# A decoder layer on one core: attention's logits in single PSUM banks, separate rings for weights and maxima, half products, and mask with maximum in one VectorE instruction

## Chip, cores and metric

One core of a Trainium2 chip runs the whole layer in one launch. The metric is device time in microseconds (us), the median of the runs shown; before the change it is 2776.85 us (three runs, 2776.67 to 2789.18). The profile is one further execution of the same kernel, with its own time.

## What is computed

The input x has 4 sequences of 1024 tokens with 256 features, and there is a context of 4 times 154 tokens. Three blocks follow each other, each with a residual:

```
x = x + liquid_scan_block(layernorm(x))
x = x + cross_attention(layernorm(x), ctx, ctx)          # 16 heads of 16, 154 keys
x = x + transformer_block(layernorm(x))                  # causal, 16 heads of 16, 1024 keys; then a mixture of experts

scores = q @ k.T / sqrt(16);  scores = where(causal, scores, -inf)   # the mask only in the transformer block
attn = softmax(scores);  o = attn @ v
w = softmax over the 2 best of 8 router logits
moe = sum_e w[e] * (gelu(h2 @ w1[e] + b1[e]) @ w2[e] + b2[e])
```

The large products are fp32. The kernel takes the softmax with the true row maximum subtracted.

## The kernel before

**Stages.** The scan block comes first (lines 166 to 574), then both attentions in one program whose TensorE order is written out by a planner (lines 600 to 1214), then the experts (lines 1230 to 1342), where the tokens, sorted by expert in DRAM, are taken in 39 blocks of 256.

**One unit of attention** is one sequence, one half of it (512 queries, called a block), and one group c of four heads out of sixteen. Heads lie 32 rows apart, so the four heads of a group are the four 32-row strips of TensorE, and two heads make a pair (strips 0 and 1, or 2 and 3). There are 32 units of cross-attention with 4 weight steps each, and 32 of self-attention, 16 with 8 steps (first half of a sequence) and 16 with 16 steps (second half). A unit has two lists of steps:

- *Maximum steps*, `few` (line 728, cross-attention) and `many` (line 744, self-attention). The logits of one pair are computed with queries on the partitions into a tile `ps_max` of two PSUM banks, one bank per head (lines 735 and 750). `many` adds the causal mask to the last 128 columns of both heads (line 755). Then VectorE reduces both heads in one instruction to the negated maximum (lines 739 and 757). `put` (line 759) transposes the four maxima of a unit and adds them to the queries as a seventeenth feature (line 766, tile `qs`), so that the second product yields logits less their maximum.
- *Weight steps*, `logits` (line 805). For a block kt of 128 keys (77 in cross-attention) and one pair, the logits are computed with keys on the partitions into a tile `ps_exp`, again two banks (line 814). ScalarE takes the exponential of both banks in one instruction into `pt` (line 816), and on the diagonal GpSimd zeroes what lies above it (line 820).
- *Products*, `weigh` (line 781): once both pairs of a key block have been issued, four matmuls, one per head, multiply `pt` with the values into the bank `ps_o` (line 788).

**PSUM.** `ps_max` and `ps_exp` share one tag, `sc`, with three tiles of two banks (line 603): six banks. `ps_o` has one bank, and one bank `mm` (line 609) serves every other matmul of attention: projections, transposes, output products, the router.

**The planner** (lines 1127 to 1214). It walks the weight steps; k counts them within a unit, so an even k is the first pair of a key block and an odd k the second. After each weight step it emits maximum steps of the next unit (`find`), kept LEAD = 3 steps ahead, so that a weight step is followed by a maximum step of the other pair. Then `fill` may emit filler: jobs of the queues `ahead` (what the next group of units needs: norms, projections) and `behind` (what follows a finished unit: `back`, output products, router), each with a lag in steps, and at most one job with matmuls per call. If `find` has just emitted a `put`, that `fill` is skipped. After an odd step it also calls `weigh` and then `fill` once more:

```
some = find(near - (near - far) * (k + 1) // n + LEAD)
left = n - k + sum(len(units[x][1]) for x in range(u + 1, limit)) - LEAD
if not some:
    fill(left)
if k % 2 and len(waiting) > 1:
    weigh()
    fill(left)
```

TensorE runs in exactly this order; ScalarE, VectorE and GpSimd are ordered by the framework's scheduler. When a group's first maxima come up, `all_ahead` emits at once what is left of `ahead`.

**Router and experts.** `route` (line 956) computes the router's logits, the gates and each token's place, and scatters the rows to DRAM. Its last four jobs per block add the experts' second bias: `turned` (line 1002) transposes the gates, `biases` (line 1008) multiplies them with the 8x256 table `eb2`, and VectorE adds the result to the residual (line 1015). In the expert loop SyncE issues for each block xr, w1, w2 and bias (lines 1312 to 1318); `results` (line 1290) computes the second product of the block before, copies it to `y` (line 1295) and scatters it.

## Time and profile before

| | us |
|---|---|
| median of three runs (2776.67 to 2789.18) | 2776.85 |
| the profiled execution | 2801.33 |
| its span, first to last instruction | 2799.6 |

| stage, from the start of the span | from | to |
|---|---|---|
| scan | 0 | 720 |
| cross-attention | 720 | 1075 |
| self-attention | 1075 | 2085 |
| last block's router, then experts | 2085 | 2800 |

| engine | busy us | share of the span | instructions |
|---|---|---|---|
| PE (matmul) | 2482.2 | 89% | 13678 |
| DVE (VectorE) | 1427.0 | 51% | 2902 |
| ACT (ScalarE) | 934.6 | 33% | 1410 |
| POOL (GpSimd) | 396.4 | 14% | 560 |

A group line of the profile reads: source line, engine, operation, tile written<-tiles read, shapes, count | busy us, mean ns of one | idle us of the engine just before them, and what ended it. A timeline line reads: start, length, engine, line, operation, tiles, shapes, count merged. An fp32 matmul of the program shows as two MATMUL records, so the two heads of a pair are four. Matmul ends are modelled, so a busy PE is not PE at its peak.

### The profile page before, as it was taken

How to read it: one execution, taken by the hardware profiler on the slowest of the kernel's cores; microseconds unless marked ns; L12 is line 12 of the kernel's file. 1: busy time of each engine (PE TensorE's matmuls, PEld its weight loads, DVE VectorE, ACT ScalarE, POOL GpSimd, SP SyncE). 2: the span in 40 equal slices, each digit the busy share in tenths (PEclk: the TensorE clock that was granted, in tenths of full speed). 3: DMA queues.
4: the chain of work that ended last, by engine and by line, in shares of the span. 5: the costliest groups of instructions: out<-in, count | busy, mean ns of one | idle time of the engine just before them, and what ended most of it. 6: DMA issues, size and time to landing. Idle time of an engine off the chain costs nothing. (4 is left out here: it accounts for less than half of the span.)

```text
span 2799.6 us, 36302 instructions
## 1 busy us (share of the span) xinstructions
PE 2482.2 (89%) x13678; PEld 1446.6 (52%) x13678; DVE 1427.0 (51%) x2902; ACT 934.6 (33%) x1410; POOL 396.4 (14%) x560
## 2 busy tenths in 40 slices
PE   5999999995898998989999999999886999999990
PEld 2666666554444554433433344333334888888880
DVE  4667766657556555575757576567733111111113
ACT  2444333432454543333423423352341222222220
POOL 1110000001101000122213131213212111111110
PEclk9999999997899999997979879897897999999995
DMA  4595000001000010100011001100003454554435
GB/s 100 112 240 138 0 1 1 0 1 26 22 19 16 22 27 16 32 11 16 8 30 40 1 10 29 39 1 24 24 1 135 166 183 167 174 187 157 172 128 181
DMA packets 138001, 186.01 MB, mean 66 GB/s; under 512 B 33513, under 2 KB 108636, under 8 KB 137820
## 3 DMA queue, kind: packets, MB, share of 16 engines
q1 hardware_dynamic: 116028, 126.32, 14.5%
q0 software_dynamic: 15264, 51.00, 7.0%
q10 hardware_dynamic: 6528, 6.29, 0.7%
q8 instruction: 111, 1.82, 0.3%
q14 instruction: 70, 0.57, 0.1%
HBM read 110.93 MB, written 61.24 MB: 61 GB/s over the span
## 5 line engine op out<-in xcount | busy, mean ns | idle before, releaser
L816 ACT ACTIVATE pt<-ps_exp 128x1024 f32<-128x1024 f32 (+4 forms) x512 | 434.6, 862 | 642.1 <-PE ps_exp L814 492.8
L814 PE MATMUL ps_exp<-qs,kT 32*128 32x512 f32 (+4 forms) x2048 | 498.4, 596 | 33.9 <-DVE mpad L757 14.7
L750 PE MATMUL ps_max<-kT,qa 32*128 32x512 f32 (+3 forms) x1536 | 402.3, 620 | 22.8 <-ACT pt L816 16.2
L757 DVE TENSOR_REDUCE mpad<-ps_max 128x2 f32<-128x1024 f32 (+3 forms) x256 | 260.3, 1020 | 133.9 <-PE ps_max L750 130.9
L1222 PE MATMUL ps<-hT,w 128*128 128x256 f32 x1248 | 288.4, 385 | 23.3 <-ACT mid L1223 21.5
L814 PEld LDWEIGHTS ps_exp<-qs,kT 32*128 32x128 f32 (+1 forms) x2048 | 158.2, 190 | 269.9 <-issue 177.0
L1228 PE MATMUL ps<-w,mid 128*128 128x256 f32 x1248 | 287.7, 379 | 0.0
L1223 ACT ACTIVATE mid<-ps,bias 128x256 f32<-128x256 f32 x312 | 139.3, 472 | 435.2 <-DMA bias<-b1s 265.6
L1222 PEld LDWEIGHTS ps<-hT,w 128*128 128x128 f32 x1248 | 233.0, 191 | 71.9 <-ACT mid L1223 36.4
L788 PE MATMUL ps_o<-pt,vs 128*32 128x512 f32 (+4 forms) x2048 | 253.2, 567 | 0.3 <-ACT oT L796 0.3
L1228 PEld LDWEIGHTS ps<-w,mid 128*128 128x128 f32 x1248 | 234.4, 190 | 30.1
L820 POOL TENSOR_SCALAR_AFFINE_SELECT pt<-pt 128x256 f32<-128x256 f32 x256 | 103.4, 408 | 670.3 <-ACT pt L816 668.8
L1295 DVE COPY y<-ps 128x256 f32<-128x256 f32 x78 | 33.1, 425 | 309.0 <-PE ps L1228 309.0
L750 PEld LDWEIGHTS ps_max<-kT,qa 32*128 32x128 f32 x1536 | 133.7, 209 | 101.2 <-ACT pt L816 68.5
L755 DVE TENSOR_TENSOR ps_max<-ps_max,mask_qk 128x256 f32<-128x256 f32 x256 | 109.3, 429 | 123.9 <-PE ps_max L750 64.2
L739 DVE TENSOR_REDUCE mpad<-ps_max 128x4 f32<-128x616 f32 x128 | 101.8, 800 | 116.2 <-PE ps_exp L814 80.6
L1297 POOL DMA_INDIRECT parts<-y,to x78 | 75.8, 972 | 527.9 <-DVE y L1295 524.0
L308 PE MATMUL ps_xz<-xnT,w_in 128*128 128x512 f32 x256 | 125.2, 606 | 0.6 <-ACT xnT L300 0.6
L325 PE MATMUL ps_a<-w,w_a 128*128 128x512 f32 x256 | 123.7, 626 | 0.0
L1320 DVE CAST to<-xr 128x2 int32<-128x2 f32 x39 | 6.6, 169 | 206.7 <-DMA parts<-y,to 186.1
L788 PEld LDWEIGHTS ps_o<-pt,vs 128*32 128x32 f32 (+1 forms) x2048 | 42.2, 112 | 128.8 <-issue 98.3
L757 DVE TENSOR_REDUCE twice<-ps_max 128x2 f32<-128x1024 f32 (+3 forms) x128 | 105.0, 823 | 3.6
(263 smaller groups left out, 3190.7 us busy)
## 6 DMA issues: line engine op xcount, KB each, us to landing
w<-in_L_ffn_e_w_dram SPq DMA_DIRECT2D x78, 1024.0 KB, 5.9
routed<-zero POOLq DMA_DIRECT2D x16, 2080.0 KB, 64.3
xr<-routed SPq DMA_DIRECT2D x39, 260.0 KB
qa<-close SPq DMA_DIRECT2D x256, 32.0 KB, 2.0
xs<-in_x_dram SPq DMA_DIRECT2D x4, 1024.0 KB, 8.8
kT<-close SPq DMA_DIRECT2D x128, 32.0 KB, 2.0
plain<-row SPq DMA_DIRECT2D x8, 512.0 KB, 3.0
z<-parts SPq DMA_DIRECT2D x16, 256.0 KB, 3.5
```

The lines of the kernel that those rows point to most:

```text
L308: nc.tensor.matmul(ps, w_in[:, k, c * P : (c + 1) * P], xnT[:, k, :], start=k == 0, stop=k == 1)
L325: nc.tensor.matmul(ps, w_a[:, k, c * P : (c + 1) * P], w[:, k, :], start=k == 0, stop=k == 3)
L750: nc.tensor.matmul(ps[:, i, : s1 - s0], qT[r, j * P : (j + 1) * P], kT[r, c, s0:s1], start=True, stop=True)
L755: nc.vector.tensor_add(x, x, mask_qk.unsqueeze(1).to_broadcast([P, 2, P]))
L757: nc.vector.tensor_reduce(to, ps[:, :, : s1 - s0], AX.X, ALU.max, negate=True)
L788: nc.tensor.matmul(o[0][g * HP : (g + 1) * HP, off:], vs[:n, kt, (4 * c + g) * HV : (4 * c + g) * HV + HP], pts[g // 2][:n, g % 2, off:], ...
L814: nc.tensor.matmul(ps[:n, i, off:], kT[r, c, k0 : k0 + n], shifted[0][r, off:], start=True, stop=True)
L816: nc.scalar.activation(pt[:n, :, off:], ps[:n, :, off:], AF.Exp, scale=HD**-0.5)
L820: nc.gpsimd.affine_select(out=x, in_=x, compare_op=ALU.is_ge, fill=0.0, base=0, pattern=[[0, 2], [1, P]], channel_multiplier=-1,)
L1222: nc.tensor.matmul(ps, w1[:, k, f * P : (f + 1) * P], hT[:, k, :], start=k == 0, stop=k == 1)
L1223: nc.scalar.activation(mid[:, f, :], ps, AF.Gelu, bias=bias[:, f : f + 1])
L1228: nc.tensor.matmul(ps, mid[:, f, j * P : (j + 1) * P], w2[:, f, :], start=f == 0, stop=f == FF // P - 1)
```

## The change

- The tag `sc` becomes two tags, `max` and `exp`, with three tiles of one bank each. Every head has its own tile, so the exponential and the maximum are taken per head: two instructions of half the width in place of one.
- In `many`, the parts that end at the diagonal get mask and maximum in one VectorE instruction per head, over the part's whole width and with its result written back to PSUM; the mask is now 512 columns wide, zero but for the last 128. The maximum is no longer negated; the sign sits in `one16`, the constant row of the keys.
- `weigh` may do only the first 256 columns and leave the rest for its next call. That is allowed for key blocks between the first and the last of a unit that lie wholly below the diagonal, and is asked for when no filler is ready.
- The planner calls `weigh` after even steps, so a key block's product is issued one step sooner. After an even step `fill` is called only when work is crowded (always in cross-attention); after an odd step it is called once, and once more only behind a second half. `weigh` empties the jobs marked soon wherever they stand in `behind`.
- `turned`, `biases` and `eb2` go. In the expert loop each block loads its expert's second bias, spread over 128 partitions, as a fifth DMA on SyncE's queue, and the copy of line 1295 becomes an addition of it. (The other branch of the program, for ties in the router, gets the same bias; it isn't run here.)

```diff
-    mask_qk = const.tile([P, P], F32, name="mask_qk")
-    make_causal_mask(nc, mask_qk, mask_val=MASK)
+    mask_qk = const.tile([P, BLK], F32, name="mask_qk")
+    nc.gpsimd.memset(mask_qk[:, : BLK - P], 0.0)
+    make_causal_mask(nc, mask_qk[:, BLK - P :], mask_val=MASK)
...
-    nc.vector.tensor_reduce(one16, ident[:, HD::HP], AX.X, ALU.add)
+    nc.vector.tensor_reduce(one16, ident[:, HD::HP], AX.X, ALU.add, negate=True)
...
             def few(j0, pair):
-                ps = ps_s.tile([P, 2, BLK], F32, tag="sc", name="ps_max")
+                pss = [ps_s.tile([P, BLK], F32, tag="max", name="ps_max") for _ in range(2)]
...
-                nc.vector.tensor_reduce(
-                    m[:, j0 : j0 + 2, 2 * pair : 2 * pair + 2, HD].rearrange("p j i -> p i j"),
-                    ps[:, :, : 2 * n].rearrange("p i (j n) -> p i j n", n=n), AX.X, ALU.max, negate=True,
-                )
+                for i in range(2):
+                    nc.vector.tensor_reduce(
+                        m[:, j0 : j0 + 2, 2 * pair + i, HD],
+                        pss[i][:, : 2 * n].rearrange("p (j n) -> p j n", n=n), AX.X, ALU.max,
+                    )
...
             def many(j, s0, pair):
-                ps = ps_s.tile([P, 2, BLK], F32, tag="sc", name="ps_max")
+                pss = [ps_s.tile([P, BLK], F32, tag="max", name="ps_max") for _ in range(2)]
...
-                if s1 == n:
-                    x = ps[:, :, s1 - s0 - P : s1 - s0]
-                    nc.vector.tensor_add(x, x, mask_qk.unsqueeze(1).to_broadcast([P, 2, P]))
-                to = twice[:, j, 2 * pair : 2 * pair + 2] if s0 else m[:, j, 2 * pair : 2 * pair + 2, HD]
-                nc.vector.tensor_reduce(to, ps[:, :, : s1 - s0], AX.X, ALU.max, negate=True)
+                for i in range(2):
+                    g = 2 * pair + i
+                    to = twice[:, j, g : g + 1] if s0 else m[:, j, g, HD : HD + 1]
+                    x = pss[i][:, : s1 - s0]
+                    if s1 == n:
+                        nc.vector.tensor_tensor_reduce(
+                            out=x, in0=x, in1=mask_qk[:, BLK - (s1 - s0) :], scale=1.0, scalar=LOWEST,
+                            op0=ALU.add, op1=ALU.max, accum_out=to,
+                        )
+                    else:
+                        nc.vector.tensor_reduce(to, x, AX.X, ALU.max)
...
-        def weigh():
-            unit, kt, n, off, pts = waiting.pop(0)
+        half_done = [False]
+        def weigh(half=False):
+            unit, kt, n, off, pts = waiting[0]
...
+            half = half and not half_done[0] and off == 0 and 0 < kt < last
+            x0, x1 = BLK // 2 if half_done[0] else off, BLK // 2 if half else BLK
             for g in range(4):
                 nc.tensor.matmul(
-                    o[0][g * HP : (g + 1) * HP, off:],
+                    o[0][g * HP : (g + 1) * HP, x0:x1],
...
-                while len(behind) and behind[0].soon and c % NCH == 1:
+                while any(x.soon for x in behind) and c % NCH == 1:
...
-                ps = ps_s.tile([P, 2, BLK], F32, tag="sc", name="ps_exp")
+                pss = [ps_s.tile([P, BLK], F32, tag="exp", name="ps_exp") for _ in range(2)]
...
-                nc.scalar.activation(pt[:n, :, off:], ps[:n, :, off:], AF.Exp, scale=HD**-0.5)
+                for i in range(2):
+                    nc.scalar.activation(pt[:n, i, off:], pss[i][:n, off:], AF.Exp, scale=HD**-0.5)
...
-            for j in range(0, NJ, 2):
-                jobs.append(Job(lambda j=j: turned(j, gTs[j // 2]), lag=1 if j else 2))
-                jobs.append(Job(lambda j=j: biases(j, gTs[j // 2]), lag=2))
...
+        def busy(left):
+            return any(q and now[0] + 1 - last[id(q)] >= q[0].lag and may(q[0]) for q in (ahead, behind))
+        def crowded(left):
+            return u < firsts[B] or 2 * (len(ahead) + len(behind)) > left or len(behind) > 12
...
-                if not some:
-                    fill(left)
-                if k % 2 and len(waiting) > 1:
-                    weigh()
-                    fill(left)
+                if k % 2 == 0:
+                    if len(waiting) > 1:
+                        weigh(not busy(left))
+                    if not some and crowded(left):
+                        fill(left)
+                else:
+                    some = (not some and fill(left)) or some
+                    if half_done[0] and len(waiting) > 1:
+                        weigh()
+                        if not some:
+                            fill(left)
...
-                        nc.vector.tensor_copy(y[:, j, :], ps)
+                        nc.vector.tensor_add(y[:, j, :], ps, last)
...
+                    last = wp.tile([P, D], F32, tag="last", name="last")
+                    nc.sync.dma_start(out=last, in_=a["L0_ffn_e_b2"][bass.ds(e, 1)].rearrange("e d -> (e d)").partition_broadcast(P))
```

## The prediction

> **What bounds the kernel now.** I read first the busy time by stage, then the page's slices, then the groups of instructions, then the timeline of one stretch. The first lines are the stages scan, cross-attention, self-attention and experts, with the busy time of each engine and the granted TensorE clock.
>
> ```profile
> 0.00:720.00 720.00, 621.15 (x2693) 398.06 (x2693) 464.53 (x890) 259.57 (x398) 63.74 (x72) 0.93 0.26 61
> 720.00:1075.00 355.00, 339.12 (x2586) 172.44 (x2584) 193.85 (x379) 170.73 (x205) 29.94 (x19) 0.99 0.09 20
> 1075.00:2085.00 1010.00, 931.17 (x5679) 375.77 (x5678) 646.37 (x1285) 361.58 (x489) 213.86 (x376) 0.87 0.07 19
> 2085.00:2800.00 715.00, 590.73 (x2724) 500.37 (x2723) 122.25 (x348) 142.74 (x318) 88.86 (x93) 0.92 0.47 162
> ```
>
> TensorE is the busiest engine everywhere, in attention above 90%; VectorE follows in self-attention with 646 of 1010 us, ScalarE has 362. The change touches the 1365 us of attention and a copy in the experts. But "busy" counts a matmul that runs alone like four that run side by side. The next lines are the groups that the change rewrites.
>
> ```profile
> L816 ACT ACTIVATE pt<-ps_exp 128x1024 f32<-128x1024 f32 (+4 forms) x512 | 434.6, 862 | 642.1 <-PE ps_exp L814 492.8
> L814 PE MATMUL ps_exp<-qs,kT 32*128 32x512 f32 (+4 forms) x2048 | 498.4, 596 | 33.9 <-DVE mpad L757 14.7
> L750 PE MATMUL ps_max<-kT,qa 32*128 32x512 f32 (+3 forms) x1536 | 402.3, 620 | 22.8 <-ACT pt L816 16.2
> L757 DVE TENSOR_REDUCE mpad<-ps_max 128x2 f32<-128x1024 f32 (+3 forms) x256 | 260.3, 1020 | 133.9 <-PE ps_max L750 130.9
> L755 DVE TENSOR_TENSOR ps_max<-ps_max,mask_qk 128x256 f32<-128x256 f32 x256 | 109.3, 429 | 123.9 <-PE ps_max L750 64.2
> ```
>
> A maximum matmul waits for an exponential (L750 <-ACT pt L816), with which it shares no data, only the PSUM slot. The timeline of a pair shows what that costs.
>
> ```profile
> 1207.12 0.70 PE L814 MATMUL ps_exp<-qs,kT 32*128 32x512 f32 x2
> 1207.13 0.70 PE L750 MATMUL ps_max<-kT,qa 32*128 32x512 f32 x2
> ...
> 1208.19 0.65 PE L835 MATMUL back<-ident,oT 128*128 128x128 f32 x4
> 1208.35 1.23 DVE L757 TENSOR_REDUCE mpad<-ps_max 128x2 f32<-128x1024 f32 x1 [0.41 <-PE ps_max L750]
> 1208.35 1.02 ACT L816 ACTIVATE pt<-ps_exp 128x1024 f32<-128x1024 f32 x1 [1.54 <-PE ps_max L750]
> ...
> 1208.77 1.13 PE L814 MATMUL ps_exp<-qs,kT 32*128 32x512 f32 x4
> 1209.43 1.13 PE L750 MATMUL ps_max<-kT,qa 32*128 32x512 f32 x4
> ...
> 1210.48 0.66 PE L835 MATMUL back<-ident,oT 128*128 128x128 f32 x4
> ...
> 1211.07 1.07 PE L788 MATMUL ps_o<-pt,vs 128*32 128x512 f32 x8
> ```
>
> The first weight step E0 and its maximum step M0 start together and take 1.07 us for both (1207.12 to 1208.19). The second pair does not: M1 starts 0.66 us after E1 (1209.43 against 1208.77), just when E0's exponential ends (1208.35 + 1.02) and gives its slot back. The shared ring of three is E0, M0, E1; M1 is the fourth. I went through the start times of all attention this way: of 118 maximum steps right behind a weight step in cross-attention 51 are late by over 0.1 us, together 38.4 us; of 340 in self-attention 147, together 124.1 us. That is **162.5 us** in which two strips run where four could.
>
> [...] The trace agrees: 1024 wide 1023 ns, 512 wide 596, 256 wide 383, two of 1024 in 1.94 us. [...] The trace agrees: 1024 wide 1223 ns, 616 wide 800, a 256-wide addition 429, so some 0.157 us + N/0.96. [...] The trace shows about 0.09 us between the end of streaming of a product or transpose and the next weight step.
>
> **The change, part by part.** I sum against the profiled execution, 2801.3 us (span 2799.6), which lies 0.9% above the median 2776.85.
>
> *Separate rings.* M1 no longer waits for an exponential, which would give 162.5 us. But a ring of three banks holds one and a half steps. The second head of a step needs the bank of the head before the last: 1.23 us from matmul to exponential (1207.12 to 1208.35), 0.60 for 512 columns, 0.06 back to TensorE, so 1.89 us after the step before; likewise about 1.23 + 0.69 + 0.06 = 1.98 for a maximum. From E0 to E1 lie 1.06 and a product of 0.99: 2.05, enough. From E1 to the next E0 lie 1.06 and a filler. A short filler (0.59 + 0.09) gives 1.74, late by 0.15 to 0.25; a projection (1.95) none; no filler 0.83 late, as E1 alone takes 1.06. A sequence of self-attention has 40 filler jobs and 8 `put`s for 48 pairs, about one per pair: some 170 pairs of 256 with a short one at 0.15, 25 us, and about 50 without at 0.56 (0.83 cut to narrower steps), 28 us. Left: 162 - 53 = **-109 us**.
>
> *Exponentials in halves.* 0.596 + 0.50 against 1.02: at most +0.17 us for each of 512 steps, up to 87 us on ScalarE. It goes from 362 + 171 to some 620 us busy in 1365, and waits for TensorE now (492.8 us); hidden. Without cover it would be the whole 87.
>
> *Maxima in halves.* `few`: 2 x (0.157 + 0.321) = 0.96 against 0.80, 128 times, +20 us. `many` without mask: 2 x 0.69 against 1.22, 128 times, +20. With mask, 256 steps of 128 to 512 columns: now 0.43 + 0.82 on average = 1.25 us; then two operations of on average 0.49 us and two accumulator reads. The trace lacks this instruction: below, the read is free, 0.98 us (-67 us in all); above, it needs two cycles per element and a read of 0.16 (the smallest VectorE instructions), 1.97 us (+184 us). I take one cycle and 0.1: 1.18 us, -16. VectorE's sum is then about +24 less 11 below; hidden except in the first-half units, where it is already 73 to 77% busy. I take 0 on the path; both ends go to the range.
>
> *Product one step sooner.* It now arrives 1.06 + filler + 1.06 us after the pair's last weight step: 2.1 us without a filler, 2.8 with one. Its exponentials are done after 1.23 + 0.60 + 0.50 = 2.33, on the diagonal 0.5 later (GpSimd, 0.41 us). Behind the waiting product stand all of TensorE's next steps. 128 of 192 products in self-attention are diagonal, but narrower: I take 0.1 us on average over 192 pairs, **+15 us** (bounds 0 and 64, at 0.5 us for each diagonal one).
>
> *Halves of products.* At most four key blocks in each of 16 units, 64. A 256-column product takes 0.57 us to the next start (at 1201.79), a whole one 0.99: 2 x 0.57 - 0.99 = 0.15, **+9 us**.
>
> *Fewer filler places.* Per sequence of cross-attention there are 28 matmul jobs; 32 steps offered up to 40 places (24 + 16), and now 24, as 8 steps carry a `put`. Two to four jobs per sequence go out in bursts, each waiting for the one bank `mm` (1.5 to 2.0 us apart at 2084 to 2092, against 0.66 inline): 10 jobs x 1.0, **+10 us** (0 to 25).
>
> *Bias out of attention.* 16 `gateT` of 0.31 us (two of 0.11 and 0.09) and 16 `bias` of 0.96 (four of 0.22 and 0.09): 20 us of TensorE. The last block's lie behind eight scatters on GpSimd (2116.7 to 2126.7) and give nothing: **-18 us**. VectorE loses 16 x 0.69 = 11 us.
>
> *Bias into the experts.* SyncE issues a fifth DMA (0.4 us) per block of 14.7 us; it stands behind `bias` and ahead of the next xr, which is used over 10 us later. 128 KB beside some 2.5 MB per block; the DMA share is 0.47. The addition (0.43) replaces a copy (0.425). 0 us; if the cover went, 39 x 0.7 = 27.
>
> *Clock.* It is 0.99 where TensorE hardly idles (cross) and 0.87 in self-attention, where it idles 79 us. Filling raises it if anything: **-15 us** (0 to -60).
>
> Sum: -109 + 15 + 9 + 10 - 18 - 15 = **-108 us**: 2693 us profiled, times 2776.85/2801.33 = **2670 us**.
>
> **Rivals.** (1) *All is regained* and the clock with it: -137 (only the short-filler loss stays), -18, half of the idle 79 us, clock -45: -240, 2538 us. For it: projections and output products are long fillers. Against it: VectorE works 3.5 us of a 4 us pair. Chance 0.12. (2) *The short ring takes most back*: one VectorE norm of 1 to 1.2 us ahead of a maximum stalls TensorE, which two whole steps of slack absorb today; and products at the upper bound. About -40: 2737 us. For it: units without maxima take 22.5 us for 16 steps now, which 1.5 steps of ring cannot better. Chance 0.20. (3) *Slower: the fused instruction is dear.* At two cycles per element a masked step costs +0.72 us. The first-half units are bound by VectorE: 128 x 0.72 = +92 on the path, and half of as much, +46, in the others, and their maxima ring waits another +20. Then -108 + 158 = +50: 2826 us. It decides from about 1.0 us for a 512-wide one, read included. For it: a kind that this trace doesn't have. Against it: one cycle per element is what every two-tensor row shows. Chance 0.15. (4) *Nothing visible*: gains and waits cancel, 2777 us. Chance 0.08. My forecast, 2610 to 2710: 0.45.
>
> **How the numbers follow.** Half a per cent, 14 us, is about what a measurement of this kernel can tell from no change. Faster: 0.45 + 0.12 + 0.20 = 0.77; same 0.08; slower 0.15. The range leaves out (3) and part of (1): 2570 to 2765.
>
> **What would show it.** Maximum steps should start with their weight step, the late ones' sum falling below some 55 us; waits of L750 for the exponential should be gone, replaced by waits for the maxima of the same ring. The fused instruction should take about 0.69 us at 512 columns; 1.0 or more would prove (3). Products waiting for `pt` by over 30 us would prove part of (2). Experts and scan should not move by 3 us. A self-attention that stays near 1010 us would make me wrong.

## The result, and the profile after

| | before | after |
|---|---|---|
| median of four runs each, us | 2776.76 (2755.95 to 2789.18) | 2911.78 (2910.59 to 2913.97) |
| profiled execution, us | 2801.33 | 2910.59 |
| its span, us, and mean granted TensorE clock | 2799.6, 0.910 | 2908.8, 0.879 |

The changed kernel is **slower by 4.9%** (ratio 1.0495, 95% interval 1.0431 to 1.0559). The forecast was 2670 us. Cut at the first weight step of cross-attention, the first one of self-attention, the last one, and the first load of an expert's rows, the two spans are:

| stage | before, us | after, us | at half clock before | at half clock after |
|---|---|---|---|---|
| scan | 726.3 | 720.0 | 105.8 | 87.8 |
| cross-attention | 384.4 | 439.7 | 17.1 | 127.2 |
| self-attention | 969.8 | 1038.6 | 259.4 | 368.0 |
| last router | 53.1 | 50.2 | 40.6 | 43.3 |
| experts | 666.0 | 660.3 | 78.9 | 80.1 |

The last two columns sum the stretches in which the trace's clock record stands at half speed; it holds only two values in both traces, 1.0 and 0.5. All of the loss lies in attention, +124 us, and there TensorE stood 219 us longer at half clock. The profile shows the same in its stages (length; then busy time of PE, its weight loads, DVE, ACT and POOL with counts; PEclk, DMA share, GB/s):

```profile
0.00:720.00 720.00, 623.07 (x2754) 399.69 (x2757) 466.23 (x903) 261.56 (x400) 67.92 (x73) 0.94 0.26 62
720.00:1159.80 439.80, 409.56 (x2677) 204.18 (x2674) 213.77 (x541) 185.38 (x342) 29.95 (x19) 0.86 0.08 17
1159.80:2198.30 1038.50, 973.92 (x5658) 392.51 (x5658) 574.98 (x1863) 376.91 (x845) 213.99 (x373) 0.82 0.06 18
2198.30:2908.80 710.50, 590.15 (x2734) 500.09 (x2731) 121.11 (x348) 143.21 (x319) 89.50 (x96) 0.91 0.51 170
```

PE is "busy" for 93 and 94% of the two attentions, before for 95 and 93% (same cut). That says little: a 512-column matmul record of one shape (32*128 32x512) took a median 588 ns at full clock and 1056 ns at half in the changed kernel (1235 and 319 records). The column that moved is PEclk, from 0.98 to 0.86 in cross-attention and from 0.87 to 0.82 in self-attention. The groups that answer to those of before:

```profile
L835 ACT ACTIVATE pt<-ps_exp 128x512 f32<-128x512 f32 (+4 forms) x1024 | 475.8, 514 | 763.0 <-PE ps_exp L833 615.3
L833 PE MATMUL ps_exp<-qs,kT 32*128 32x512 f32 (+4 forms) x2048 | 604.9, 636 | 10.5 <-ACT pt L835 8.8
L754 PE MATMUL ps_max<-kT,qa 32*128 32x512 f32 (+3 forms) x1536 | 489.7, 619 | 29.7 <-DVE mpad L767 10.4
L762 DVE CUSTOM_DVE_ANT_0 ps_max<-ps_max,mask_qk 128x256 f32<-128x256 f32 (+3 forms) x512 | 242.6, 513 | 230.8 <-PE ps_exp L833 126.8
```

The trace shows the program's `tensor_tensor_reduce` (line 762) as two records under names of its own, CUSTOM_DVE_ANT_0 for the masked maximum (710 ns at 512 columns) and DVE_READ_ACCUMULATOR2_ANT for the read of the accumulator (142 ns).

The maximum matmul (now L754) no longer waits for an exponential but for a maximum of its own ring, as the prediction said it would. And the maximum steps do start with their weight step: the late ones' sum fell from 162.5 to 64.7 us (counted in the stages of the table: 14.4 in cross-, 50.3 in self-attention). The overlap was regained, and the time rose. Whether the separate rings regained it is another question, which e5 and e6 answer below.

Where self-attention falls to half clock is seen at 1427.5 us, near the end of the second unit of a first half. First VectorE, then TensorE (start, length, engine, line, operation, tiles, shapes, count, and idle time before with what ended it):

```profile
1423.34 0.86 DVE L115 TENSOR_SCALAR r_h<-mv_h 128x4 f32<-128x4 f32 x1
...
1425.58 1.47 DVE L133 TENSOR_SCALAR row<-v,mv_h,r_h 128x256 f32<-128x256 f32 x4 [1.05 <-POOL r_h L116]
1426.97 0.69 DVE L762 CUSTOM_DVE_ANT_0 ps_max<-ps_max,mask_qk 128x512 f32<-128x512 f32 x1
1427.58 0.14 DVE L762 DVE_READ_ACCUMULATOR2_ANT mpad<- 128x1 f32 x1
```

```profile
1424.45 0.38 PE L833 MATMUL ps_exp<-qs,kT 32*128 32x128 f32 x2
1424.47 0.69 PE L754 MATMUL ps_max<-kT,qa 32*128 32x512 f32 x1
1424.67 0.28 PE L833 MATMUL ps_exp<-qs,kT 32*128 32x128 f32 x2
1425.00 0.59 PE L754 MATMUL ps_max<-kT,qa 32*128 32x512 f32 x1
1427.77 1.22 PE L754 MATMUL ps_max<-kT,qa 32*128 32x512 f32 x1 [2.18 <-DVE mpad L762]
```

The router's norm sits ahead of the maxima on VectorE, 1.05 us of waiting for GpSimd and 1.47 of work. The ring of three banks holds one and a half steps and runs out; TensorE stands 2.18 us, and meanwhile the clock falls to half, for 58.0 us. The same stall comes in sequences 3 and 4 (2.17 and 2.99 us, then 58.0 and 20.5 us).

My **theory** from here, not yet shown: the time is lost by TensorE's clock, which falls where the array is little used and comes back only with dense work of the whole array; the short rings and the new order of products and fillers make such places. The **rivals**: the rings' waits cost the time by themselves; or the earlier and halved products do; and the clock is only a sign.

### The profile page after: what moved, and what is told of

Its sections match the earlier page's. It is cut to its first block, busy times and chain, and to the rows that moved or that the text cites. A ratio compares the mean times of both kernels' runs of the same rounds, so it can differ in the third digit from the quotient of the medians.

```text
span 2908.8 us, 37780 instructions
## 1 busy us (share of the span) xinstructions
PE 2596.7 (89%) x13814; PEld 1496.5 (51%) x13814; DVE 1376.1 (47%) x3654; ACT 967.1 (33%) x1906; POOL 401.4 (14%) x561
## 4 chain that ended last, share of the span: by engine, by line
PE 58%; issue 22%; DVE 11%; POOL 5%; ACT 3%; DMA 2%; SPq 0%; POOLq 0%; DVEq 0%; ACTq 0%
PE ps_exp L833 14%; PE ps_o L802 9%; PE ps_max L754 7%; PE proj L700 4%; PE ps_xz L310 3%; PE ps_a L327 3%; POOL parts L1311 3%; PE wo L873 2%; PE z L441 2%; PE ps_max L738 2%; PE ps_o L548 2%; PE shift L774 2%; PE tp L687 2%; PE back L854 1%; PE vals L713 1%
## 5 line engine op out<-in xcount | busy, mean ns | idle before, releaser
L835 ACT ACTIVATE pt<-ps_exp 128x512 f32<-128x512 f32 (+4 forms) x1024 | 475.8, 514 | 763.0 <-PE ps_exp L833 615.3
L833 PE MATMUL ps_exp<-qs,kT 32*128 32x512 f32 (+4 forms) x2048 | 604.9, 636 | 10.5 <-ACT pt L835 8.8
L754 PE MATMUL ps_max<-kT,qa 32*128 32x512 f32 (+3 forms) x1536 | 489.7, 619 | 29.7 <-DVE mpad L767 10.4
L762 DVE CUSTOM_DVE_ANT_0 ps_max<-ps_max,mask_qk 128x256 f32<-128x256 f32 (+3 forms) x512 | 242.6, 513 | 230.8 <-PE ps_exp L833 126.8
L833 PEld LDWEIGHTS ps_exp<-qs,kT 32*128 32x128 f32 (+1 forms) x2048 | 196.3, 197 | 293.5 <-issue 242.0
L802 PE MATMUL ps_o<-pt,vs 128*32 128x256 f32 (+4 forms) x2280 | 289.3, 561 | 22.7 <-POOL pt L839 22.1
L754 PEld LDWEIGHTS ps_max<-kT,qa 32*128 32x128 f32 x1536 | 181.2, 213 | 94.3 <-DVE mpad L767 31.3
L767 DVE TENSOR_REDUCE mpad<-ps_max 128x1 f32<-128x512 f32 x256 | 166.0, 686 | 126.4 <-PE ps_max L754 124.8
L743 DVE TENSOR_REDUCE mpad<-ps_max 128x2 f32<-128x308 f32 x256 | 111.1, 475 | 146.5 <-PE ps_exp L833 138.2
L738 PE MATMUL ps_max<-kT,qa 32*128 32x154 f32 x1024 | 125.1, 354 | 7.8 <-DVE mpad L743 7.7
```

Of the source, the lines that this page charges most:

```text
L738: nc.tensor.matmul(pss[i][:, (j - j0) * n : (j - j0 + 1) * n], qT[r, j * P : (j + 1) * P], kT[r, c, :n], start=True, stop=True,)
L754: nc.tensor.matmul(pss[i][:, : s1 - s0], qT[r, j * P : (j + 1) * P], kT[r, c, s0:s1], start=True, stop=True)
L762: nc.vector.tensor_tensor_reduce(out=x, in0=x, in1=mask_qk[:, BLK - (s1 - s0) :], scale=1.0, scalar=LOWEST, op0=ALU.add, op1=ALU.max, accu ...
L767: nc.vector.tensor_reduce(to, x, AX.X, ALU.max)
L802: nc.tensor.matmul(o[0][g * HP : (g + 1) * HP, x0:x1], vs[:n, kt, (4 * c + g) * HV : (4 * c + g) * HV + HP], pts[g // 2][:n, g % 2, x0:x1] ...
L833: nc.tensor.matmul(pss[i][:n, off:], kT[r, c, k0 : k0 + n], shifted[0][r, off:], start=True, stop=True)
```

## The experiments

Ratios are against runs of the kernel before beside it on the same chip. These had medians from 2762.6 to 2805.8 us, so ratios, not times, compare the kernels. "Half" is half-clock time from the first weight step to the first expert load, in the profile. "Clock" is the mean granted clock of the timed executions, in brackets that of the executions of the kernel before that the ratio uses. For the changed kernel's own partner only the profiled execution has a clock on record.

| run | ratio, 95% interval | span, us | half, us | clock (before) |
|---|---|---|---|---|
| before | 1 | 2799.6 | 317 | 0.910 in the profile |
| changed kernel | 1.0495 (1.043 to 1.056) | 2908.8 | 538 | 0.878 |
| e1 new tiles, old order | 1.029 (1.024 to 1.034) | 2825.5 | 329 | 0.908 (0.923) |
| e2 old tiles, new order | 1.030 (1.026 to 1.034) | 2841.4 | 327 | 0.908 (0.923) |
| e3 warm | 1.0595 (1.054 to 1.065) | 2911.2 | 463 | 0.888 (0.923) |
| e4 row norm on GpSimd | 1.0618 (1.057 to 1.067) | 2938.9 | 562 | 0.877 (0.923) |
| e5 shared ring | 1.0105 (1.003 to 1.018) | 2827.8 | 421 | 0.894 (0.910) |
| e6 shared ring, old order | 0.985 (0.977 to 0.994) | 2760.4 | 268 | 0.920 (0.910) |
| e7 bias only | 0.982 (0.975 to 0.990) | 2768.4 | 303 | 0.919 (0.910) |
| e8 no halves | 1.0455 (1.038 to 1.053) | 2939.8 | 563 | 0.877 (0.910) |
| e9 warm, quarter of the array | 1.076 (1.071 to 1.081) | 2987.7 | 643 | 0.867 (0.922) |
| e10 early products | 1.0305 (1.027 to 1.034) | 2853.5 | 317 | 0.915 (0.922) |
| e11 filler places | 1.0225 (1.020 to 1.026) | 2820.9 | 329 | 0.910 (0.922) |
| e12 bias only, warm | 0.993 (0.990 to 0.996) | 2749.8 | 242 | 0.927 (0.922) |
| e13 four and two banks | 1.085 (1.079 to 1.091) | 2984.3 | 604 | 0.867 (0.924) |
| e14 two and four banks | 1.0695 (1.064 to 1.075) | 2952.8 | 633 | 0.865 (0.924) |
| e15 bias only, once more | 0.991 (0.987 to 0.994) | 2757.3 | 300 | 0.927 (0.924) |
| e16 bias only, warm, once more | 0.997 (0.995 to 0.999) | 2755.4 | 245 | 0.926 (0.924) |

**The change in two halves: e1 and e2.** e1 puts the old loop into the changed kernel; e2 puts the new `weigh`, `fill` and loop into the kernel before.

```diff
-                if k % 2 == 0:
-                    if len(waiting) > 1:
-                        weigh(not busy(left))
-                    if not some and crowded(left):
-                        fill(left)
-                else:
-                    some = (not some and fill(left)) or some
-                    if half_done[0] and len(waiting) > 1:
-                        weigh()
-                        if not some:
-                            fill(left)
+                if not some:
+                    fill(left)
+                if k % 2 and len(waiting) > 1:
+                    weigh()
+                    fill(left)
```

> The changed kernel with the order of the kernel before: products after odd steps only, never in halves, filler places as they were. One-bank rings, fused mask and maximum and the moved bias stay. Theory (the new order, with the rings of one and a half steps, lets TensorE run dry for 1.5 to 3 us at a few places, the clock halves and returns only with the next dense full-array filler; 495 us at half clock in cross- and self-attention against 277 before): more fillers in place keep the clock, half-clock time falls to about 300 us and the time to 2700 to 2780 us. Rival A (the one-bank rings by themselves cost the time, in waits for the row's own predecessor): it stays above 2860 us whatever the order. Rival B (the earlier, halved products are what costs): below 2760 us with the half-clock time unchanged.

> The kernel before with the new order alone: products after even steps too, in halves where asked for, and the new filler places; shared ring of three two-bank tiles, old mask and maximum, bias in attention. Theory: two whole steps of slack stay in the ring, so the norms don't stall TensorE by 2 us, but the fillers still come in bunches: 2790 to 2850 us. Rival A (rings): 2777 us or faster, as the order costs nothing. Rival B (products): 2850 to 2920 us, all of the loss.

Each half costs 3%. That refutes both rivals as the sole cause, and a part of the theory too: e1 lies above the theory's range, and e2, within it, has hardly more half-clock time in its profile than the kernel before in its own (327 against 317 us), yet it is 42 us longer. But the profiled execution of the kernel before stood at a low clock for that kernel, 0.910. Beside e1 and e2 its timed executions had 0.923, and these two 0.908. So each half costs clock as well; an estimate of how much follows below. What the order costs besides is waiting: TensorE idles 127 us of attention in e2, before 93. The products head its waits (what waited for what, us in total, times, longest), where the list of the kernel before has no product at all:

```profile
PE ps_o L792 <- POOL pt L828: 39.3, 16, 6.7
...
PE back L843 <- DVE on L847: 12.4, 11, 2.1
```

The first is a product that comes before GpSimd's select is done, the second fillers in a row on the one bank `mm`.

**Is the clock a cause? e3 and e9.** Both add 28 products to the changed kernel at the starts of seven units; in e3 they use all 128 rows of the array, in e9 32.

```diff
+        def heat(n):
+            ps = mm_tile("heat")
+            for _ in range(n):
+                nc.tensor.matmul(ps, ident, mask_qk, start=True, stop=True)              # e3
+                nc.tensor.matmul(ps, ident[:HP], mask_qk[:HP], start=True, stop=True)    # e9
...
             for k, job in enumerate(weigh_jobs):
+                if k == 0 and u in (0, 42, 50, 58, 60, 62, 63):
+                    heat(4)
                 job()
```

> The changed kernel with work added: four products of the 128x128 identity with 512 columns of the mask, their result unused, at the start of seven units (the first of cross-attention; the third first-half unit of sequences 2, 3 and 4; the first, third and fourth second-half unit of sequence 4), all of which lie in or just behind a long stretch at half clock. 28 products of 0.95 us at full and 1.9 us at half clock are 27 to 53 us of added TensorE work. Theory (clock): the stretches of 48 to 58 us end after 4 to 8 us, some 200 to 270 us of half clock go, and the kernel is 50 to 110 us faster than without the added work, 2800 to 2860 us. Rivals (waits or earlier products cost the time, and the clock is only a sign of it): 25 to 55 us slower, 2935 to 2965 us.

> As the warm run, 28 added products of 512 columns at the same seven places, but with 32 of the 128 rows of the array (one strip in place of four), so that TensorE streams as long and a quarter of the array works. In the warm run the first four ended the 54.6 us at half clock at the start of cross-attention after 10.2 us, and cross-attention fell from 439.7 to 420.3 us. Theory (what brings the clock back is a stretch in which the whole array works, not one in which TensorE is merely busy): the stretch at the start of cross-attention stays at 48 us or more, cross-attention takes 440 us or more, and the whole is at least as slow as with whole-array products, 2925 to 2980 us. Rival (the clock follows how much of the time TensorE streams): as the warm run, the stretch ends within 14 us and cross-attention takes about 420 us.

The start of cross-attention, in stretches of 15 us, in the changed kernel, in e3 and in e9:

```profile
714.00:729.00 15.00, 14.92 (x82) 9.85 (x82) 7.98 (x17) 3.33 (x6) 0.00 (x0) 0.50 0.09 21
729.00:744.00 15.00, 15.00 (x78) 6.75 (x78) 4.15 (x9) 5.10 (x9) 0.00 (x0) 0.50 0.01 1
744.00:759.00 15.00, 15.00 (x84) 7.31 (x81) 4.15 (x9) 5.58 (x11) 0.00 (x0) 0.50 0.06 15
759.00:774.00 15.00, 15.00 (x92) 7.20 (x86) 4.74 (x10) 5.75 (x11) 0.00 (x0) 0.67 0.03 7
```

```profile
714.00:729.00 15.00, 14.82 (x72) 8.35 (x70) 5.95 (x13) 2.40 (x5) 0.00 (x0) 0.68 0.08 19
729.00:744.00 15.00, 14.73 (x135) 6.90 (x132) 7.37 (x17) 8.77 (x17) 0.00 (x0) 1.00 0.04 12
744.00:759.00 15.00, 15.00 (x130) 8.43 (x128) 7.27 (x16) 8.33 (x17) 0.00 (x0) 1.00 0.05 12
```

```profile
714.00:729.00 15.00, 13.95 (x68) 8.72 (x67) 7.03 (x15) 1.97 (x2) 0.00 (x0) 0.65 0.16 36
729.00:744.00 15.00, 14.32 (x70) 7.36 (x72) 4.24 (x9) 4.46 (x9) 0.00 (x0) 0.50 0.00 0
744.00:759.00 15.00, 15.00 (x81) 6.87 (x76) 4.15 (x9) 5.24 (x10) 0.00 (x0) 0.50 0.03 8
```

In the changed kernel PE is busy 15.00 of 15 us, and the clock stands at 0.50 all the same. Four whole-array products bring 1.00, and the next 15 us hold 135 matmuls in place of 78. Four products of the same length on a quarter of the array bring nothing: the stretch lasts 61.4 us. Cross-attention takes 439.7 us as changed, 420.3 in e3, 442.7 in e9. In self-attention the third first-half units of sequences 2 and 3, unchanged instructions, took 28.9 us, all of it at half clock, and 15.9 with none in e3: **0.45 us for each microsecond at half clock**. But the whole of e3 was not faster; its 2923 us lie between the two forecasts. Half clock moved to places that had been free of it (51.2 and 54.6 us of it from the last unit of sequences 2 and 3 on, which went from 28.5 to 44.9 and 46.4 us). The clock is a cause; a few added products are no cure.

The kernel before gives a second price, without any edit. Its 60 timed executions beside these experiments have clocks from 0.900 to 0.936 and times from 2826.3 to 2733.1 us; a line through them falls by 27 us per 0.01 of clock (correlation -0.97; 19 to 25 us within each of the four sets). It fits the first price: at 0.45 us each, 0.01 of the mean clock of a 2770 us kernel, some 55 us at half clock, is 25 us.

With that line the losses can be split, as an estimate. Before the change the line has 0.918 at the median of 2776.8 us; the changed kernel has 0.878. The difference is worth some 107 of the 135 us, or 75 at the smallest of the four slopes (the line is drawn past the clocks that it was fitted on). Most of the loss is clock, then, and some 28 us are left. Of the mean losses of e1 and e2, 75 and 82 us, the clock is some 41 each and the rest 34 and 41. The two halves don't add: together they cost more clock than one by one, and less besides.

**The trigger: e4.** `rows` calls the norm with its last four instructions on GpSimd.

```diff
-                norm(u[:, :, :D], vb, NJ, "h2")
+                norm(u[:, :, :D], vb, NJ, "h2", nc.gpsimd)
```

> The changed kernel with the four subtract-and-scale instructions of the router's norm (1.47 us on VectorE, behind 1.05 us of waiting for GpSimd) on GpSimd, so that they don't stand ahead of the maxima on VectorE. Theory (a VectorE norm ahead of the maxima stalls TensorE 2.2 to 3.0 us in the second first-half unit of sequences 2, 3 and 4, and that stall halves the clock for 20 to 58 us): those three stalls fall below 1 us, two or three of the 58 us stretches go, 40 to 90 us faster than the changed kernel: 2820 to 2870 us. Rival (the stalls are only their own 2 to 3 us each, the clock falls for another reason): within 10 us of 2912 us, the long stretches stay.

The forecast is refuted, but the edit tests the stall in one place only. In sequence 3 the stall is gone (the longest idle time just before the fall is 0.63 us, where it was 2.17), and the clock falls all the same, for 20.5 us and, some 10 us later, for 58.0. So there a smaller lull does as well. In sequence 2 a stall of 3.20 us behind a masked maximum remains. In sequence 4 the fall comes during a new one of 3.80 us: a product waits for GpSimd's select. GpSimd now carries the norm, and the products' waits for it rose from 22.1 to 37.6 us, so e4 has a cost of its own.

**The rings: e5, e6, e13, e14.** e5 gives weights and maxima one ring of six one-bank tiles; e6 has the old loop of e1 as well.

```diff
-                pss = [ps_s.tile([P, BLK], F32, tag="max", name="ps_max") for _ in range(2)]
+                pss = [ps_s.tile([P, BLK], F32, tag="sc", name="ps_max", bufs=6) for _ in range(2)]
...
-                pss = [ps_s.tile([P, BLK], F32, tag="exp", name="ps_exp") for _ in range(2)]
+                pss = [ps_s.tile([P, BLK], F32, tag="sc", name="ps_exp", bufs=6) for _ in range(2)]
```

> The changed kernel with one ring of six one-bank tiles for weights and maxima together, in place of three and three; all else as changed. Theory (a ring of three banks, one and a half steps, is too short: a unit without maxima takes 28.5 us against 22.5, the fourth first-half unit 108 us in all against 92 at full-clock worth, and VectorE's norms stall TensorE by 2 to 3 us, which halves the clock): units without maxima go back to 22 to 24 us, the 58 us stretches at half clock at the end of the second first-half unit go, self-attention falls by 40 to 90 us and the time to 2810 to 2870 us, although some maximum steps are late again (60 us summed now, 100 to 160 then). Rival (separate rings gain what was forecast, and the loss lies in the order): late maxima add their 70 to 100 us, 2950 us or more.

> One ring of six one-bank tiles, and the order of the kernel before as well; what is left of the change is the fused mask and maximum, the instructions per head and the moved bias. Theory (ring length and order are each some 70 us of loss, the rest is a small gain): 2740 to 2780 us, the bias and the fused instruction gaining up to 25 us, single-head maxima giving some back. Rival (the per-head instructions cost the time in the new-tiles-old-order run): 2820 us or more.

Both times lie where the theory said: sharing takes 3.9 points off the changed kernel, and 4.4 off e1. Self-attention falls from 1038.6 to 951.8 us, while cross-attention rises from 439.7 to 450.8. By the same line e5 lost 44 us to the clock, more than the 30 us that it lost in all, so that the rest is a gain of some 13. Of e6's gain of 40 us, 27 are clock and 13 the rest.

Two things I had wrong. First, the late maxima stay at 66.9 us in e5, not 100 to 160. So it was not the separation that made them start in time. With the old order they sum to 126.3 us in the shared ring (e6) and 104.0 in separate ones (e1), with the new order to 66.9 and 64.7: separation is worth 2 to 22 us of the 162.5. The order alone brings 130.4 (e2), single banks and instructions per head 126.3 (e6), both together 66.9 (e5). And e6, with 126.3 us of late maxima, is no faster than e7, which has 167.0 and the old tiles: there the regained overlap shows in no time, unless the instructions per head cost as much as it gained. Second, the stall behind the norm stays. At the end of the second first-half unit of sequence 2 TensorE stands 3.88 us in e5, now in `put`, for the bank `mm` that VectorE frees behind norm and maxima. The 58 us stretches did go; there the clock falls for 20.5 us.

e13 and e14 keep two rings but shift a bank between them (`bufs=2` for the maxima and `bufs=4` for the weights, and the reverse).

> The changed kernel with four banks for the weights and two for the maxima. Theory (both rings at one and a half steps are short, and lending is what counts): units without maxima go from 28.5 us to 22 to 25 us, but with one step of ring for the maxima a fourth first-half unit, which has two maximum steps per weight step, waits for VectorE each time and lengthens; 2930 to 3020 us in all. Rival (the weights' ring is the short one): the units without maxima shorten and nothing else lengthens, 2880 us or less.

> The changed kernel with two banks for the weights and four for the maxima. Theory (as above): the stalls of 2 to 3 us behind VectorE's norms at the end of the second first-half unit go, but each weight step waits for the exponential of the step before: 1.89 us from step to step, so units without maxima take 30 to 36 us; 2900 to 3000 us in all. Rival (the maxima's ring is the short one, by the norms' stalls and the clock that falls with them): 2870 us or less.

Lengths in sequence 1 of the two units in which one ring bears all (half-clock time in brackets; the last unit has eight maximum steps for sixteen weight steps, and is the one that the expectations call a unit without maxima):

| banks for weights, maxima | fourth first-half unit, us | last unit, us |
|---|---|---|
| before: three two-bank tiles, shared | 25.9 (0) | 22.5 (0) |
| changed: 3, 3 | 31.6 (0) | 28.5 (0) |
| e5: 6 shared | 23.8 (0) | 25.0 (0) |
| e13: 4, 2 | 43.3 (19) | 26.1 (0) |
| e14: 2, 4 | 23.8 (0) | 47.5 (41) |

Neither ring is the short one: each is short where its steps come in a row, and two rings can't lend. e5's last unit, at 25.0 us, missed the 22 to 24 that I expected, and e13's, at 26.1, the 22 to 25. e14 lost more than I expected of its last unit, since the clock fell in it, and the stall that should have gone is there (3.67 us in sequence 2, as in e5). Of the 6 us that the last unit lost, the ring took 3.5 (28.5 against 25.0), and the order some 3 to 4 (e6 with the old order took 21.2, and e2 25.4 against 22.5); the new tiles in a shared ring by themselves gained about 1. The timeline of that unit before and after:

```profile
1337.60 0.70 PE L814 MATMUL ps_exp<-qs,kT 32*128 32x512 f32 x2
1337.62 0.49 PE L750 MATMUL ps_max<-kT,qa 32*128 32x128 f32 x4
1338.07 1.13 PE L814 MATMUL ps_exp<-qs,kT 32*128 32x512 f32 x6
1339.13 1.06 PE L788 MATMUL ps_o<-pt,vs 128*32 128x512 f32 x8
```

```profile
1379.48 0.64 PE L802 MATMUL ps_o<-pt,vs 128*32 128x256 f32 x8
1380.05 1.13 PE L833 MATMUL ps_exp<-qs,kT 32*128 32x512 f32 x4
1381.11 0.64 PE L802 MATMUL ps_o<-pt,vs 128*32 128x256 f32 x8
```

Before, the two pairs of a key block lie next to each other and run side by side in four strips: eight records and a narrow maximum step within 1.53 us (1337.60 to 1339.13), and then the product. After, half a product stands between the pairs, and each has its 1.06 us alone in two strips (1380.05 to 1381.11).

**The parts of the order: e10, e11, e8.** e10 and e11 are the kernel before with one part each; e8 is the changed kernel with `weigh()` for `weigh(not busy(left))`.

```diff
+                if k % 2 == 0 and len(waiting) > 1:     # e10
+                    weigh()
                 if not some:
                     fill(left)
-                if k % 2 and len(waiting) > 1:
-                    weigh()
+                if k % 2:
                     fill(left)
...
-                if not some:                            # e11
+                if not some and (k % 2 or crowded(left)):
                     fill(left)
                 if k % 2 and len(waiting) > 1:
                     weigh()
-                    fill(left)
```

> The kernel before with one thing changed: a key block's product is issued after the next even step instead of the next odd one, one step sooner. Tiles, halves and filler places as before. The prediction's term was 15 us (0 to 64). Theory (TensorE waits in order for exponentials and GpSimd's selects, 40 us more in products in the run with the new order alone): 25 to 50 us slower than before, most of that run's 3.0%. Rival (the filler places are what the order costs): within 10 us of before.

> The kernel before with one thing changed: the filler places of the new order (after even steps only when crowded, after odd ones once). Products as late as before and whole. The prediction's term was 10 us (0 to 25). Theory (jobs bunch up at the ends of groups, cross-attention above all, and the stretches without a whole-array filler let the clock fall): 20 to 45 us slower than before, cross-attention 405 to 430 us against 384. Rival (early products are what the order costs): within 10 us of before.

> The changed kernel with no product in halves; a key block's product is issued whole after the even step. The prediction's step was 9 us for the halves. Theory (the halves are a small matter beside ring and order): within 25 us of the changed kernel's 2912 us on either side, the clock deciding the sign. Rival (halves split the dense stretches and so hold the clock down): 2860 us or less.

Early products cost 3.05%, filler places 2.25%, both together 3.0% (e2): each more than I expected, and not a sum. In e10 two fillers follow each other after an odd step, so part of its loss is bunching too. In their profiles half-clock time is 317 and 329 us, but beside the kernel before on the same chip their clock was lower by 0.007 and 0.012, an estimated 18 of 81 us and 31 of 56. TensorE idles 145 and 113 us of attention in these profiles, before 93, so the larger part of e10's loss is waiting, and about a third of e11's. Whole products in place of halves changed nothing that the two intervals can tell apart.

**The bias, and the clock once more: e7, e12, e15, e16.** e7 is the kernel before with `turned`, `biases` and `eb2` removed and the bias added in the experts; e12 adds `heat(4)` to it at units 9, 16, 42 and 50. e15 and e16 are the same two side by side on one chip.

> The kernel before with the second bias moved to the experts, nothing else. The prediction's step was -18 us, from 20 us less TensorE work in attention. Theory (fillers also keep the clock up, and the router's queue behind is 4 jobs shorter per block): -20 to +10 us, 2745 to 2775 us. Rival (the bias jobs were what kept the clock up late in each sequence, so that their going costs): +15 us or more.

> The bias-only kernel with four products of the 128x128 identity with 512 constant columns, their result unused, at the start of four units in which it stood at half clock for 24 to 41 us (the tenth and seventeenth of cross-attention, the third first-half unit of sequences 2 and 3). 16 products are 15 to 30 us of added work. Theory (clock): some 90 of these 133 us at half clock go, which is worth 0.45 us each, 40 us, less 15 to 25 us of work: 10 to 30 us faster than the bias-only kernel, ratio 0.970 to 0.980. Rival (the fall only moves to a later place, as in self-attention in the warm run): 0 to 20 us slower, ratio 0.983 to 0.990.

> The bias-only kernel once more, on the chip of the next run, so that the two can be compared: it measured a ratio of 0.982 on a chip where the kernel before took 2806 us, and 0.980 to 0.995 is expected here.

> The bias-only kernel with 16 added whole-array products at the start of four units, beside the same without. In profiles the two stood at 2749.8 and 2768.4 us, with 242 and 303 us at half clock from attention's start to the experts. Theory (a microsecond less at half clock is worth some 0.45 us; 61 of them 27 us, less 16 products of 0.95 us, 15 us): 5 to 25 us faster than without, although work is added. Rival (added work can only cost; the difference was that of the chips): 10 to 25 us slower.

The bias alone gains: 0.982 (0.975 to 0.990), and 0.991 (0.987 to 0.994) in e15. e12, at 0.993, missed both forecasts. The profile of the bias-only kernel in e7 shows 61 us more at half clock than that of e12, but side by side e16 was slower than e15, 2750.3 against 2727.9 us (0.997 against 0.991), and the rival was right. The reason shows in the clocks of the timed executions: their mean was 0.927 without the added products and 0.926 with them, so that of the 22 us between them the added work alone, 16 products of an estimated 0.95 us (a projection of two such products took 1.98 us), is some 15. The profiled execution of e15 was its slowest, 2759.0 us at 0.914; the products were added against half-clock time that its other executions mostly didn't have. No version with parts of the new tiles or the new order beat the bias alone; e6 matches it.

## Why the prediction was wrong, step by step

- **Separate rings, -109 us: failed, the largest error.** The late maxima did fall to about what was forecast (53 us forecast, 64.7 measured), but not because the rings were separate: with one ring of six banks they fall to 66.9 (e5). And the term took each microsecond of late start for one of time, while e6 beside e7 shows no gain from 41 us less of it. On the other side, "Left" counted only short fillers and missing ones, at 0.15 and 0.56 us. Against a shared ring of as many banks the separation costs 3.9 and 4.4% (e5, e6), some 105 to 120 us (72 to 76 between the plain medians, from different chips). Of that an estimated 63 to 68 us is clock. The direct part shows in the units where one list of steps stands alone. The stall behind the norm is no part of what is shown, since it stays with six banks.
- **Clock, -15 us, "Filling raises it if anything": failed.** It fell from 0.910 to 0.879 in the profiles; at 27 us per 0.01 that is an estimated 84 of the 109 us between them, and 107 of 135 between the medians. I read the clock as following idle time. TensorE's idle time in attention hardly rose (93 to 95 us by the modelled ends), and the clock fell. This error and the one above overlap, as most of what the rings and the order cost is clock.
- **Product one step sooner, +15, and filler places, +10: right in sign, far too small.** Alone 3.05% and 2.25%, together 3.0%, some 84 us of 2777. The working priced the wait for exponentials and selects at 0.1 us a pair; in e2 16 waits for a select take 39.3 us, the longest 6.7. It priced fillers in a row on one bank in cross-attention only. And it left out that a product between two pairs ends their side-by-side run, and the clock.
- **Halves, +9:** not told apart from nothing (1.0455 against 1.0495).
- **Bias out of attention, -18:** right: 0.9% and 1.8%, or 25 and 44 us between the mean times. The clock is an estimated 6 and 23 of them; the rest, 19 and 21, is what the term said.
- **Bias into the experts, 0; exponentials and maxima in halves, 0:** right. The experts took 660.3 against 666.0 us. An exponential took 1023 ns at 1024 columns before and 597 at 512 after, a plain maximum 1223 and 686. With the old order and a shared ring, all per-head instructions together stand at 0.985 beside 0.982 without them, on the same chip.
- **Fused instruction:** 0.71 us at 512 columns and 0.14 for the read of the accumulator, against 0.69 and 0.1 assumed. The "cycle" of the working, 1.04 ns, is the slope between maxima of 1024 and 616 columns before (1223 and 800 ns). Rival (3) is refuted: VectorE's total fell from 1427.0 to 1376.1 us. The kernel got slower, but not for that reason.
- **Rival (2), the short ring**, came nearest: it named the unit of 22.5 us that a ring of one and a half steps can't better, and products at their upper bound. Its sum for the whole change was -40 us between profiles, where +109 was measured. It had no term for the clock, and the norm that two steps of slack should absorb stalls TensorE with six banks too.

What the clock follows can be asked of the traces. The half-clock stretches last 3.4, 6.8, 10.2, ... 54.6, 58.0 us, and in each of the two profiles, before and after, the clock's changes lie on one grid of 3.41 us. I cut attention into windows of that length and estimated from the matmuls' columns, at some 0.95 ns each (a projection's four records of 512 take 1.98 us together) and twice that at half clock, how long TensorE streamed (took in columns on at least one strip) and what share of the array, rows times columns, was in use on average. In the changed kernel at half clock, TensorE streamed a median 0.94 of the windows that stayed so, and 0.98 of those after which the clock rose: no great difference. The array's share was 0.63 and 0.93. At full clock the share was 0.68 where the clock stayed and 0.33 where it fell; but streaming fell too, from 0.93 to 0.43, so it is the returns that tell the two measures apart, not the falls. The estimates for the eighteen profiles of this case, all of closely related kernels, taken together:

| array's share in a window | fell from full clock | rose from half clock |
|---|---|---|
| below 0.35 | 260 of 271 windows | 0 of 164 |
| 0.35 to 0.5 | 152 of 514 | 0 of 192 |
| 0.5 to 0.9 | 0 of 4255 | 196 of 1352 |
| above 0.9 | 0 of 479 | 225 of 225 |

With 0.5 to 0.9 of the array in use the clock mostly kept the state that it had: 0 of 4255 windows fell and 196 of 1352 rose. 5607 of the 7452 windows lie there, and so one lull can cost tens of microseconds, as the 58.0 us behind the stall of 2.18 us. Two rings of three had a lower clock than one of six (0.878, against 0.894 in e5) at the same TensorE idle time in attention (95 and 93 us), so idle time doesn't tell the two apart.

What stays open: the split of the +135 us into some 107 of clock and 28 of the rest is an estimate from one line. It is open, too, what e1's direct loss consists of, as TensorE idles less there than before (72 against 93 us in attention); that its matmuls more often run alone is likely but not shown. And it is open whether the array's share is what the clock follows: e9 supports it, the window figures are an estimate.

## What to carry to other kernels

Before a shared ring of buffers is split, look for the stretches in which one user stands alone: there the ring has only its own part (28.5 us against 25.0 in the last unit of a sequence here). Before an order of instructions is changed, look at what ran side by side by being next to each other. And read PEclk beside PE's busy share in each stage, not idle time alone: a TensorE that is busy all the time with part-array matmuls can stand at half clock (15.00 of 15 us busy at 0.50 in the changed kernel), where each microsecond held some 0.45 us of loss here. Where two kernels are compared by their profiles, see first where each profile's clock lies among the timed executions.

## What was not expected of the hardware

- The half clock's persistence: 45 us on end at PEclk 0.50 with PE busy 44.92 of them (714 to 759 us of the changed kernel). With four whole-array products the stretch lasted 10.2 us in place of 54.6, with four of 32 rows 61.4.
- One execution of an unchanged kernel differs from the next mainly by its clock: 60 executions, 2733 to 2826 us, on one line of 27 us per 0.01. A single profile may stand at one end of it, as that of the kernel before did (0.910).
- The masked maximum with accumulator costs no more per column than the plain maximum: 710, 581 and 445 ns at 512, 384 and 256 columns, some 1.04 ns a column, as 1223 and 800 ns at 1024 and 616 columns before. The read of the accumulator adds 142 ns.
